# A gated recurrence over a graph on one core: where its states, sums and late rows are kept

## The chip, the core and the metric

The kernel runs on one NeuronCore of a Trainium2 chip. The metric is the device time of one execution in microseconds (us); of several executions the median is taken. The core has TensorE (PE, matmuls, weight loads as PEld), VectorE (DVE), ScalarE (ACT), GpSimd (POOL) and SyncE (SP), which here only issues transfers. A name with q at its end (SPq, ACTq) is the engine's sequencer, which also issues DMAs.

## What is computed

Four graph layers over x [64 batches, 256 nodes, 256 features] and a weighted adjacency [64, 256, 256], each followed by a residual sum and a layer norm. Only layer 0 is touched by the change:

```python
d = adj.sum(-1); norm_adjT = swapaxes(adj, 1, 2) * where(d != 0, 1 / d, 0)[:, :, None]
def step(h, i):                       # i = 0 .. 255, one after the other
    x = h_e[:, i]
    x_par = einsum('bj,bjd->bd', norm_adjT[:, i], h)
    r, z = sigmoid(split(x @ W_ioux.T + b_ioux + x_par @ W_iouh.T + b_iouh))
    hc = tanh(x @ W_coux.T + b_coux + (x_par * r) @ W_couh.T + b_couh)
    return h with row i = z * x_par + (1 - z) * hc
```

h starts as the input, so row i of the sum takes new states for nodes before i and old features (x) for nodes from i on. Layers 1 to 3 are a graph convolution and two attention layers; each batch goes through them alone.

## The kernel before, in words

`_recurrence` does layer 0 and leaves its states in DRAM (Hd); `_layers` does the rest. 64 batches times two halves of 128 features fill the 128 partitions, so that one state, one gate or one sum of a step is a 128x128 tile.

A step n is a chain: the sum xp is transposed on TensorE and copied to SBUF by ScalarE (`flip`, L442 to L447); `h_part` multiplies it by the gate weights; ScalarE forms r (L581), VectorE r times xp (L582); a second flip, a second `h_part`, tanh (L615); then VectorE makes the next sum from c, the gate and what is ready of the sum (v, L600 and L601; xp, L619 and L620). The new state h is formed at the start of the next step (L536, L537).

The sum over nodes is split by age. Time is in blocks of 32 nodes (T), and rounds of 8 (U).

- Pushes. A new state is multiplied by an adjacency weight and added to the sums (ACC) of the nodes in its own round and the next: one instruction of VectorE for a target (`push`, L462), while GpSimd takes the last few targets together (`far`, L566 and L570). The two engines work beside each other. A step has up to 9 pushes of VectorE.
- Late sums. Once a round, TensorE adds what the states of the last 48 or so nodes give to the eight nodes of the round after the next (`late`, L366). It reads a ring Hw in SBUF of 64 rows of states, in two halves of 32 batches. Each state first goes to DRAM (L538); once a round eight rows are read back into the ring (L333). The products are copied (L179) to lb, where a target row lies in one partition, sent to DRAM (Lb, L343), read back (late_sb, L349) in the layout of ACC, and added by GpSimd (L633). The eight rows of a round lie next to each other in each 32 partitions of lb.
- Early sums. For each block, 256 rows times 32 targets of each batch: states older than that and all the old x rows (`early`, L252). They go to DRAM (Eb), and from there to ACC.
- Degrees (`degrees`, L198 to L210) and tables S, An for a block are made one block ahead.

The order of the loop is written out by hand (`manual_schedule`). By p = n % 8: the late matmuls are put in at p = 1 (two pieces after the gates' matmuls) and at p = 2, 3, 4 (one piece ahead of the first gate's matmuls, one behind the second's); early pieces take the same two places at p = 0, 5, 6, 7. Copies wait in a list (`copy_next`), two to a step; loads on ScalarE's queue (L624) and transfers on SP's come at the end of a step. SP sends lb at the end of p = 5 and reads it back at p = 6. GpSimd's addition is put at the end of p = 6, and the first push at p = 7 needs it. Every DMA issue takes one of eight landing counters in turn and waits until the transfer that had it before has landed. [...]four for products and transposes (base), two for rc (the gate r and the candidate c), one for z and one for `flip`.

Of the kernel before, what the change touches and what calls it, by code (L numbers as in the profile page):

```python
# [69 lines left out]
def _recurrence(tc, ident, Hd, x, adj, W_ioux, b_ioux, W_iouh, b_iouh, W_coux, b_coux, W_couh, b_couh):  # L70
# [15 lines left out]

    nc = tc.nc
# [6 lines left out]
    GB = 8  # L94
    NG = B // 4
# [3 lines left out]
    with ExitStack() as ctx:  # L99
# [6 lines left out]
        tri = const.tile([P, T], F32, name="tri")  # L106
# [49 lines left out]
        for s in range(0, P, T):  # L156
            nc.gpsimd.affine_select(
                out=tri[s:s + T], in_=tri[s:s + T], pattern=[[-1, T]], compare_op=ALU.is_ge,
                fill=0.0, base=0, channel_multiplier=1,
            )  # L160

# [3 lines left out]
        dram = ctx.enter_context(tc.tile_pool(name="r_dram", bufs=2, space=bass.MemoryType.DRAM))  # L165
# [3 lines left out]
        copies = []  # L169
        loads = []  # L170
        transfers = {}

        def copy_later(out, in_, then=None):
            copies.append((out, in_, then))

        def copy_next(n):
            if copies:
                out, in_, then = copies.pop(0)
                nc.scalar.copy(out, in_)  # L179
                if then:  # L180
                    then(n)

        def transfer_at(n, f):
            transfers.setdefault(n, []).append(f)

        def base_bank(shape, name):
            return ps.tile(shape, F32, tag="base", name=name, bufs=4)
# [24 lines left out]
        def early_A(k, t, n=None):  # L212

            A = stream.tile([P, 2, 2 * GB, T], F32, tag="A", name=f"A_{k}_{t}")
            g = slice(t * GB, (t + 2) * GB)
            new, own = k * T - W + T // 2, k * T
            for at in range(max(new, 0) // T * T, own, T):
                nc.gpsimd.memset(A[at % P:at % P + T, at // P], 0.0)
            for jc in range(2):
                lo, hi = jc * P, (jc + 1) * P  # L220
                for a, b in ((lo, min(new, hi)), (max(own, lo), hi)):
                    if a < b:
                        nc.sync.dma_start(
                            A[a - lo:b - lo, jc],
                            adj[g, a:b, k * T:(k + 1) * T].rearrange("b j i -> j b i"),
                        )
            def cut():
                part = A[own % P:own % P + T, own // P]
                nc.gpsimd.tensor_mul(  # L229
                    part, part,  # L230
                    tri[own % P:own % P + T].unsqueeze(1).to_broadcast([T, 2 * GB, T]),
                )

            transfer_at(n + 2, cut) if n is not None else cut()
            return A

        def early_H(k, t, queue=False):

            Hs = stream.tile([P, 2, GB, D], F32, tag="Hs", name=f"Hs_{k}_{t}")
            g = slice(t * GB, (t + 1) * GB)  # L240
            new = k * T - W + T // 2
            for jc in range(2):
                lo, hi = jc * P, (jc + 1) * P
                for src, a, b in ((Hd, lo, min(new, hi)), (x, max(new, lo), hi)):
                    if a < b:
                        to, of = Hs[a - lo:b - lo, jc], src[g, a:b, :].rearrange("b j d -> j b d")
                        loads.append((to, of)) if queue else nc.scalar.dma_start(to, of)
            return Hs

        def early_piece(pb, n, jc, t, A, Hs):  # L250
            for q in range(4):
                nc.tensor.matmul(  # L252
                    pb[q * T:(q + 1) * T, n, :], A[:, jc, t % 2 * GB + n * 4 + q, :],
                    Hs[:, jc, n * 4 + q, :], start=(jc == 0), stop=(jc == 1),
                )

        def early_out(Eb, eb, t):
            for q in range(4):
                nc.sync.dma_start(
                    Eb[2 * t - 6:2 * t + 2, q].rearrange("n i d -> i n d"), eb[q * T:(q + 1) * T]  # L260
                )

        def early_in(k, Eb):
            ACC = blk.tile([P, T, P], F32, tag="ACC", name=f"ACC_{k}")
            for c in range(2):
                nc.sync.dma_start(
                    ACC[c * B:(c + 1) * B],
                    Eb.rearrange("n q i d -> (n q) i d")[:, :, c * P:(c + 1) * P],
                )
            tables[k]["ACC"] = ACC  # L270

        def early_Eb(k):
            return dram.tile([NG, 4, T, D], F32, tag="Eb", name=f"Eb_{k}")

        def early_eb(k, t):
            return stream.tile([P, 8, D], F32, tag="eb", name=f"eb_{k}_{t}", bufs=1)

        def early(k):

            Eb = early_Eb(k)  # L280
            n = yield
            A = [early_A(k, 0, n)]
            Hs = [early_H(k, t, True) for t in range(2)]
            n = yield
            for t in range(B // GB):
                m = t * 2 % 8
                if m == 0:
                    eb = early_eb(k, t)
                if t % 2 == 0 and t + 2 < B // GB:
                    A.append(early_A(k, t + 2, n))  # L290
                pb = base_bank([P, 2, D], f"early_{k}_{t}")
                for piece in range(4):
                    early_piece(pb, piece // 2, piece % 2, t, A[t // 2], Hs[t])
                    if piece == 3:
                        then = None
                        if m == 6:
                            def then(n, t=t, eb=eb):
                                transfer_at(n, lambda: early_out(Eb, eb, t))
                                if t == B // GB - 1:
                                    transfer_at(n + 1, lambda: early_in(k, Eb))  # L300
                        copy_later(eb[:, m:m + 2, :], pb, then)
                        if t + 2 < B // GB:
                            Hs.append(early_H(k, t + 2, True))
                    n = yield

        def late_load(k, n=None):

            An = blk.tile([P, HB, T], F32, tag="An", name=f"An_{k}")
            first, last = k * T - W + T // 2, k * T + T // 2
            if first < 0:  # L310
                nc.gpsimd.memset(An, 0.0)
            for lo, hi, at in ring(max(first, 0), last):
                for g in range(2):
                    nc.sync.dma_start(
                        An[g * W + at:g * W + at + hi - lo],
                        adj[g * HB:(g + 1) * HB, lo:hi, k * T:(k + 1) * T].rearrange(
                            "b j i -> j b i"
                        ),
                    )

            def cut():
                nc.gpsimd.tensor_mul(An, An, window[k % 2].unsqueeze(1).to_broadcast([P, HB, T]))

            transfer_at(n + 3, cut) if n is not None else cut()
            return An

        def late(first):
# [3 lines left out]
            for lo, hi, at in ring(max(first - 2 * U, 0), first - U):  # L331
                for g in range(2):
                    nc.sync.dma_start(  # L333
                        Hw[g * W + at:g * W + at + hi - lo],
                        Hd[g * HB:(g + 1) * HB, lo:hi, :].rearrange("b j d -> j b d"),
                    )
            lb = stream.tile([P, NG, D], F32, tag="lb", name=f"lb_{first}", bufs=1)
            Lb = dram.tile([NG, 4, U, D], F32, tag="Lb", name=f"Lb_{first}")
            sides[first] = blk.tile([P, U, P], F32, tag="late", name=f"late_sb_{first}")

            def send():
                for q in range(4):
                    nc.sync.dma_start(  # L343
                        Lb[:, q].rearrange("n i d -> i n d"), lb[q * T + i:q * T + i + U]
                    )
# [8 lines left out]
            def then(n):  # L354
                transfer_at(n, send)
                transfer_at(n + 1, receive)

            yield
            for u in range(0, NG // 2, 2):
                pb = [base_bank([P, 2, D], f"late_{first}_{u}_{g}") for g in range(2)]  # L360
                for e in range(2):
                    for q in range(4):
                        for g in range(2):
# [3 lines left out]
                                pb[g][q * T:(q + 1) * T, e, :], An[rows, b, :], Hw[rows, b, :],  # L367
                                start=True, stop=True,
# [8 lines left out]
                    yield  # L377

        def load_S(k):
# [3 lines left out]
            for c in range(2):  # L383
                nc.sync.dma_start(
                    S[c * B:(c + 1) * B, U - lag:],
                    adj[:, k * T - lag:(k + 1) * T, k * T:(k + 1) * T],
                )
# [15 lines left out]
        def load_x(q):  # L403
            xq = stream.tile([P, Q, P], F32, tag="xq", name=f"xq_{q}")
            for c in range(2):
                nc.sync.dma_start(
# [65 lines left out]
        for k in range(2):  # L472
            for _ in degrees(k):
                pass
# [515 lines left out]
```

## Time and profile before

| what | us |
|---|---|
| median of 3 runs (5433.3 to 5439.5) | 5435.06 |
| the profiled execution | 5423.65 |
| its span | 5421.8 |

The span in three stages, by busy time of the engines, granted TensorE clock and bytes moved:

| stage, us from the start | PE | DVE | ACT | POOL | clock | GB/s |
|---|---|---|---|---|---|---|
| 0 to 182.5: before the first step | 48.6 | 24.3 | 11.2 | 29.5 | 0.82 | 195 |
| 182.5 to 2718.9: the steps | 1546.7 | 1502.7 | 565.5 | 723.3 | 0.79 | 95 |
| 2718.9 to 5421.8: last step's end and the layers | 2446.3 | 1535.0 | 1285.8 | 774.3 | 0.95 | 27 |

A line of a wait names who waited, for what, the total in us, how often and the longest. A line of the timeline has the start, the time it took, the engine, the line and what it writes and reads; what stands in brackets is idle time ahead of it. A line of the chain gives the start and the length of one link of what ended last.

### The profile page before, as it was taken

What the parts mean: (1) busy time and instruction counts of PE and PEld (TensorE: products, weight loads), DVE (VectorE), ACT (ScalarE), POOL (GpSimd) and SP (SyncE); (2) the same over time, 40 slices, a digit from 0 to 9 for tenths busy, and PEclk for the clock granted to TensorE, in tenths of its full rate; (3) what the DMA queues carried; (4) which work ended last, traced back from release to release, by engine and by line L of the source; (5) the groups of instructions that cost most, each with busy time, mean ns of one, the idle gap of its engine ahead of it and who ended that gap; (6) DMA issues with size and microseconds to landing.
All of it is one profiled execution on the core that took longest, in us unless ns stands there. A gap on an engine that the chain in (4) does not pass through costs nothing.

```text
span 5421.8 us, 86877 instructions
## 1 busy us (share of the span) xinstructions
PE 4041.6 (75%) x31904; PEld 2685.1 (50%) x31904; DVE 3062.1 (56%) x9234; ACT 1862.5 (34%) x5755; POOL 1527.0 (28%) x1735
## 2 busy tenths in 40 slices
PE   2566655566565565666669999999999999999998
PEld 1333333333332333333356666666666666666665
DVE  1456656556465564666645655555565555555554
ACT  0122222122121221222234445444444544444454
POOL 1222222223222222232322222222322232232221
PEclk8777778778777787877889999999999999999999
DMA  7434555645545455432110001000000000000000
GB/s 198 100 85 96 110 116 110 125 99 105 115 103 130 94 117 106 98 65 39 32 61 28 24 24 31 25 24 28 28 24 24 30 26 24 28 28 24 24 22 9
DMA packets 571745, 349.86 MB, mean 65 GB/s; under 512 B 200876, under 2 KB 563128, under 8 KB 571320
## 3 DMA queue, kind: packets, MB, share of 16 engines
q1 hardware_dynamic: 449936, 224.23, 19.6%
q10 hardware_dynamic: 121384, 120.08, 8.7%
q8 instruction: 252, 4.13, 0.3%
q14 instruction: 173, 1.42, 0.1%
HBM read 277.49 MB, written 66.58 MB: 63 GB/s over the span
## 4 chain that ended last, share of the span: by engine, by line
PE 40%; DVE 24%; DMA 23%; POOL 4%; ACT 3%; issue 3%; SPq 2%; ACTq 0%; DVEq 0%; POOLq 0%
DVE ACC L462 10%; DMA Hw<-Hd 6%; DMA Lb<-lb 5%; PE tr L720 5%; PE o L909 4%; PE mm_3f L735 3%; DMA late_sb<-Lb 3%; PE rc L429 3%; PE mm_2f L735 2%; PE mm_2k L735 2%; PE mm_2s L735 2%; DMA ad<-in_adj_dram 2%; PE rc L437 2%; PE mm_3q L735 2%; PE mm_2q L735 2%
## 5 line engine op out<-in xcount | busy, mean ns | idle before, releaser
L462 DVE SCALAR_TENSOR_TENSOR ACC<-h,S,ACC 128x128 f32<-128x128 f32 x1867 | 959.2, 571 | 411.3 <-POOL ACC L633 402.3
L750 ACT ACTIVATE sm<-sm,mx 128x256 f32<-128x256 f32 x1152 | 574.4, 500 | 520.8 <-DVE mx L746 509.3
L444 PE MATMUL rT_ps<-ident,r 128*128 128x128 f32 x256 | 95.5, 373 | 650.7 <-DVE r L582 650.6
L566 POOL TENSOR_TENSOR far<-h,S 128x512 f32<-128x512 f32 (+2 forms) x253 | 212.1, 838 | 1211.6 <-DVE h L537 1211.2
L720 PE MATMUL tr<-ident,sm 128*128 128x128 f32 x2304 | 412.5, 303 | 156.5 <-ACT sm L750 155.6
L446 ACT COPY rT<-rT_ps 128x128 f32<-128x128 f32 x256 | 67.9, 265 | 1124.7 <-PE rT_ps L444 1124.0
L720 PEld LDWEIGHTS tr<-ident,sm 128*128 128x128 f32 x2304 | 290.6, 152 | 309.9 <-ACT sm L750 258.9
L746 DVE CUSTOM_DVE_ANT_0 sm<-s,neg 128x256 f32<-128x256 f32 x1024 | 377.4, 416 | 104.7 <-PE s L869 104.7
L444 PEld LDWEIGHTS rT_ps<-ident,r 128*128 128x128 f32 x256 | 38.9, 152 | 778.6 <-DVE r L582 749.8
L366 PE MATMUL late<-Hw,An 64*32 64x256 f32 x3968 | 213.9, 454 | 261.1 <-DMA Hw<-Hd 261.1
L708 POOL TENSOR_TENSOR rstd<-rstd,mhalf 128x2 f32<-128x2 f32 x256 | 179.0, 699 | 767.0 <-DVE rstd L707 594.9
L429 PE MATMUL rc<-WxT,xqT 128*64 128x256 f32 x2048 | 389.2, 465 | 0.0
L909 PE MATMUL o<-pT,v 128*32 128x256 f32 x2048 | 322.5, 410 | 19.4 <-ACT pT L727 14.3
L619 DVE SCALAR_TENSOR_TENSOR xp<-c,Sd,zc 128x128 f32<-128x128 f32 x255 | 89.6, 351 | 434.9 <-ACT c L615 431.5
L727 ACT COPY pT<-tr 128x512 f32<-128x512 f32 x448 | 250.9, 577 | 72.9 <-PE tr L720 72.7
L710 DVE TENSOR_SCALAR y<-y,mv,rstd 128x256 f32<-128x256 f32 x512 | 189.3, 412 | 142.1 <-POOL rstd L708 142.1
L252 PE MATMUL early<-Hs,A 128*32 128x256 f32 x2048 | 170.6, 429 | 126.5 <-POOL A L229 60.6
L570 POOL TENSOR_TENSOR ACC<-ACC,far 128x512 f32<-128x512 f32 (+2 forms) x253 | 252.0, 996 | 19.8
L366 PEld LDWEIGHTS late<-Hw,An 64*32 64x32 f32 x3968 | 59.5, 117 | 332.2 <-DMA Hw<-Hd 286.7
L750 ACT ACTIVATION_READ_ACCUMULATOR sm<-sm,mx 128x1 f32 x1152 | 217.0, 188 | 0.0
L704 DVE BATCH_NORM_STATS2 st<-y 128x6 f32<-128x256 f32 x512 | 194.5, 412 | 17.8 <-POOL y L793 9.9
L437 PE MATMUL rc<-WhT,xpT 128*64 128x128 f32 x2048 | 173.2, 291 | 38.1 <-ACT xpT L446 37.8
(158 smaller groups left out, 8596.3 us busy)
## 6 DMA issues: line engine op xcount, KB each, us to landing
Hs<-in_x_dram ACTq DMA_DIRECT2D x48, 1024.0 KB
rows<-in_adj_dram SPq DMA_DIRECT2D x128, 128.0 KB
xq<-in_x_dram SPq DMA_DIRECT2D x128, 128.0 KB
Eb<-eb SPq DMA_DIRECT2D x64, 256.0 KB
ACC<-Eb SPq DMA_DIRECT2D x16, 1024.0 KB
Hd<-h SPq DMA_DIRECT2D x256, 64.0 KB
Hs<-Hd ACTq DMA_DIRECT2D x16, 1024.0 KB
y<-Hd SPq DMA_DIRECT2D x64, 256.0 KB
```

The lines of the kernel that those rows point to most:

```text
L366: nc.tensor.matmul(pb[g][q * T:(q + 1) * T, e, :], An[rows, b, :], Hw[rows, b, :], start=True, stop=True,)
L429: nc.tensor.matmul(G[o * B:(o + 1) * B], xqT[n // Q][:, n % Q, kc * B:(kc + 1) * B], WxT[:, kc, o, gates], start=False, stop=False, skip_g ...
L437: nc.tensor.matmul(G[o * B:(o + 1) * B], hT[:, kc * B:(kc + 1) * B], WhT[:, kc, o, g], start=False, stop=(kc == 1), skip_group_check=True,)
L462: nc.vector.scalar_tensor_tensor(acc[:, 0, :], h, s, acc[:, 0, :], ALU.mult, ALU.add)
L566: nc.gpsimd.tensor_mul(tmp[:, 0:len(far), :], h.unsqueeze(1).to_broadcast(shape), s.unsqueeze(2).to_broadcast(shape),)
L570: nc.gpsimd.tensor_add(acc, acc, tmp[:, 0:len(far), :])
L720: nc.tensor.transpose(pt[:, a, c * P:(c + 1) * P], src[:, c, a * P:(a + 1) * P], ident)
L727: copy(dst, flipped(src, t))
L735: nc.tensor.matmul(pm[:, c, :], lhsT[:, k, c * P:(c + 1) * P], rhs[:, k, :], start=(k == 0), stop=(k == 1),)
L746: nc.vector.tensor_tensor_reduce(out=dst[:, c, :], in0=src[:, c, :], in1=neg[:, c, :], scale=-scale, scalar=FMAX, op0=ALU.add, op1=ALU.min ...
L750: nc.scalar.activation(dst[:, c, :], dst[:, c, :], AF.Exp, bias=mx, scale=-1.0, accum_out=sums)
L909: nc.tensor.matmul(o_ps[i * HD:(i + 1) * HD], v[:, k, h * HD:(h + 1) * HD], pT[i][:, k, :], start=(k == 0), stop=(k == 1),)
```

## The change

`_layers` is the same. In `_recurrence`:

- The x side of the sums is split off. Ahead of the loop, the products of x with the adjacency are formed for all targets up to node 127 of every batch and written to DRAM (Us); the other half is formed in the first blocks of the loop, at the early places (`x_side`). Early sums now hold states alone, in eight pieces of up to 112 rows (`early`), added by VectorE to a part of Us that is loaded for it and written back. ACC is loaded from Us. Degrees ahead of the loop are made for one block, not for two.
- New states go to the ring within SBUF: ScalarE copies h to hs, and two DMAs write its two feature halves into one row of each half of the ring (`into_ring`). The ring's reload goes. Hd is written from the ring, 32 rows once a block (`flush`). For steps 17 to 20 of a block the writes are held back.
- h, zx and the product sc lie in one PSUM bank (keep); r, c and z are formed in place in PSUM; base has three banks. Each VectorE instruction of a step but the flips' sources has one operand in PSUM. GpSimd no longer forms zx; it forms ready, the finished sum times dinv.
- The late products' columns are arranged so that a round's eight rows lie four partitions apart in lb. late_sb has one buffer.
- Loads of S, An's raw rows, A and Hs wait in one list for ScalarE's queue.

```diff
+        Us = dram.tile([4, N, NG, D], F32, name="Us", bufs=1)
...
+            for g in range(0, B, GB):
...
+                for jc in range(2):
+                    rows = slice(jc * P, (jc + 1) * P)
+                    nc.sync.dma_start(A[:, jc], adj[g:g + GB, rows, 0:P].rearrange("b j i -> j b i"))
+                    nc.scalar.dma_start(Xs[:, jc], x[g:g + GB, rows, :].rearrange("b j d -> j b d"))
...
+                    x_out(0, g + n, 4, ub)
...
+        def sums_in(k, n):
...
+                    nc.sync.dma_start(
+                        ACC[c * B + q:(c + 1) * B:4],
+                        Us[q, k * T:(k + 1) * T, :, c * P:(c + 1) * P].rearrange("i n d -> n i d"),
+                    )
...
+                def add(n):
+                    nc.vector.tensor_add(U_sb[:, m:m + 2], U_sb[:, m:m + 2], pb)
...
         def late(first):
...
-            for lo, hi, at in ring(max(first - 2 * U, 0), first - U):
-                for g in range(2):
-                    nc.sync.dma_start(
-                        Hw[g * W + at:g * W + at + hi - lo],
-                        Hd[g * HB:(g + 1) * HB, lo:hi, :].rearrange("b j d -> j b d"),
-                    )
...
-                        Lb[:, q].rearrange("n i d -> i n d"), lb[q * T + i:q * T + i + U]
+                        Lb[:, q].rearrange("n i d -> i n d"),
+                        lb[q * T + i // U:(q + 1) * T:T // U],
...
                 nc.vector.scalar_tensor_tensor(
-                    acc[:, 0, :], h, s, acc[:, 0, :], ALU.mult, ALU.add
+                    acc[:, 0, :], keep[:, j % 2, :], s, acc[:, 0, :], ALU.mult, ALU.add
                 )
...
+        def flush(lo, hi):
...
+                    nc.sync.dma_start(
+                        Hd[g * HB:(g + 1) * HB, lo:hi, :].rearrange("b j d -> j b d"),
+                        Hw[g * W + at:g * W + at + hi - lo],
+                    )
+
+        def state(n):
+
+            h = keep[:, n % 2, :]
+            zcc = new("zcc", n)
+            nc.vector.tensor_mul(zcc, zc, c)
+            nc.vector.tensor_add(h, zcc, keep[:, 2, :])
+            hs = new("hs", n, 6)
+            nc.scalar.copy(hs, h)
+            ring_in.append((n, hs))
+
+            if not 0 < (n + 1) % T - T // 2 < 5:
+                into_ring()
+            return hs
+
+        def into_ring():
+            while ring_in:
+                n, hs = ring_in.pop(0)
+                for o in range(2):
+                    nc.sync.dma_start(
+                        Hw[n % W::W, :, o * P:(o + 1) * P], hs[o * B:(o + 1) * B]
+                    )
...
-                h = new("h", n - 1, 4)
-                nc.vector.tensor_mul(h, zc, c)
-                nc.vector.tensor_add(h, h, zx)
-                nc.sync.dma_start(Hd[:, n - 1, :].rearrange("b (c f) -> c b f", c=2), h)
+                hs = state(n - 1)
...
+                ready = new("ready", n)
+                nc.gpsimd.tensor_mul(
+                    ready, tables[kk]["ACC"][:, ii, :], dinv[:, n + 1:n + 2].to_broadcast([P, P])
+                )
+            push(3)
...
-            nc.gpsimd.tensor_mul(zx, z, xp)
+            zx = keep[:, 2, :]
+            nc.vector.tensor_mul(zx, Gz, xp)
...
-                nc.vector.scalar_tensor_tensor(v, z, Sd[:, ii:ii + 1], xp, ALU.mult, ALU.mult)
-                nc.vector.scalar_tensor_tensor(
-                    v, tables[kk]["ACC"][:, ii, :], dinv[:, n + 1:n + 2], v, ALU.mult, ALU.add
-                )
-                push(5)
+                nc.vector.scalar_tensor_tensor(v, zx, Sd, ready, ALU.mult, ALU.add)
+                push(4)
+                next_of(sums, n)
...
-                nc.vector.scalar_tensor_tensor(xp, c, Sd[:, ii:ii + 1], zc, ALU.mult, ALU.mult)
-                nc.vector.tensor_add(xp, xp, v)
+                nc.vector.scalar_tensor_tensor(sc, c, Sd, zc, ALU.mult, ALU.mult)
+                nc.vector.tensor_add(xp, sc, v)
...
+            if i == 16:
+                flush(n - T, n)
```

## The prediction

> **What bounds the kernel now.** I read the 40 slices first: the four layers are two stages, and only the first one, the recurrence, is touched. Then when steps start (the operations on xpT_ps), the waits between 200 and 2711 us, one step in the timeline, and the chain of one late round.
>
> ```profile
> PE   2566655566565565666669999999999999999998
> ...
> PEclk8777778778777787877889999999999999999999
> ...
> L462 DVE SCALAR_TENSOR_TENSOR ACC<-h,S,ACC 128x128 f32<-128x128 f32 x1867 | 959.2, 571 | 411.3 <-POOL ACC L633 402.3
> ```
> ```profile
> L444 PE MATMUL xpT_ps<-ident,xp x256: 272/328/476, 182.5 to 2718.9; 128*128 128x128 f32 x128
> ```
> Step 0 starts at 182.5 us, step 255 at 2718.9: 2536.4/255 = 9.95 us a step, 79.6 us per eight. What follows takes 5421.8 - 2718.9 = 2702.9 us.
> ```profile
> POOL ACC L633 <- DMA late_sb<-Lb: 436.8, 31, 20.2
> DVE ACC L462 <- POOL ACC L633: 402.3, 31, 18.2
> ...
> PEld late L366 <- DMA Hw<-Hd: 286.7, 59, 10.1
> ```
> Each eight steps VectorE waits 402.3/31 = 13.0 us for the late sums' return through DRAM (Lb), and TensorE about 286.7/31 = 9.2 us for the ring's reload (Hw).
> ```profile
> 441.46 2.83 DVE L462 SCALAR_TENSOR_TENSOR ACC<-h,S,ACC 128x128 f32<-128x128 f32 x4
> 441.51 0.82 POOL L566 TENSOR_TENSOR far<-h,S 128x384 f32<-128x384 f32 x1 [3.24 <-DVE h L537]
> ...
> 442.41 1.00 POOL L570 TENSOR_TENSOR ACC<-ACC,far 128x384 f32<-128x384 f32 x1
> ...
> 445.06 1.13 DVE L462 SCALAR_TENSOR_TENSOR ACC<-h,S,ACC 128x128 f32<-128x128 f32 x4
> ...
> 453.64 0.33 PE L444 MATMUL xpT_ps<-ident,xp 128*128 128x128 f32 x1
> ...
> 458.85 0.33 PE L444 MATMUL xpT_ps<-ident,xp 128*128 128x128 f32 x1
> ```
> Four pushes take 2.83 us beside GpSimd and 1.13 alone; a step with little on GpSimd takes 5.21 us.
> ```profile
> 454.00 9.60 DMA Lb<-lb
> ...
> 464.31 6.83 DMA late_sb<-Lb
> ...
> 471.30 2.35 POOL ACC L633
> ...
> 482.14 5.10 DMA Hd<-h
> ...
> 487.37 7.30 DMA Hw<-Hd
> ```
> So 79.6 = 22.2 of waits + 57.4, or 7.2 a step: 5.2 clean, 2.0 of stretched VectorE work and half clock.
>
> [...] The trace [...]shows no push with a PSUM operand. [...] 128x512 with a PSUM source (L787) and without (L840) both take 692 ns. I take nothing, at most 0.2 us a step.
>
> **The change, part by part.**
>
> *Start.* Out go two blocks of early sums, two of degrees and Eb; in come the x sums of all 64 batches (8.4 MB of adjacency, 16.8 MB of x, 8.4 MB written to Us), one block of degrees, and 2.1 MB back. About 38 MB against 34 MB, in longer runs, but degrees now queue behind it all. At the 265 GB/s of the best early slices 33.6 MB take 127 us; with 38 us of setup before and 20 for degrees and tables after: 185 us (165 to 230), as before.
>
> *VectorE and GpSimd.* Every push reads h from PSUM, and zcc, h, rx, zx, v, sc and xp have at most one SBUF input. 571 - 347 ns (mean less median) x 1867 = 418 us of VectorE time goes, 1.6 us a step, where the chain waits for VectorE. GpSimd loses zx (0.49 us) and gains ready (same shape). ScalarE gains the copy hs, 0.27 us, beside TensorE's work. A push waits for hs, some 0.3 us; then four pushes (1.1 us) end about 0.4 us after the gate r is there. A step is 4.9 (5.21 less the 0.3 that the gate waited for VectorE at 455.5) + 0.4 + 0.1 for PSUM = 5.4 at full clock. Half clock, about 1.7 us in a step, held some 40% of the recurrence (granted 0.75 to 0.83); I leave 0.3, since 0.7 is the share as before and a clock that is always full gives none. 5.7 x 256 = 1459 us (1360 to 1560).
>
> *Ring.* The DRAM round trip per eight steps (5.10 + 7.30 us, 9.2 of it waited) goes. But in the built order, late matmuls at steps p = 1 to 4 read all 64 ring rows and so wait for the row written in that very step; at p = 2, 3, 4 they stand ahead of the gate matmuls on TensorE. After xp, h takes 0.6 us, hs 0.35, the first of two issues 0.5 (Hd<-h: median 0.534). No trace shows such a transfer within SBUF; Hd<-h took 4.0 to 5.2 us from h, issue included. I bound the second one at 3.0 (half the rows, no DRAM) to 4.5 us from its issue, so 4.45 to 5.95 after xp. Then 0.66 of late matmuls, and gates that would start at 0.9 start at 5.1 to 6.6. I take 4.6 us lost at each of p = 2, 3, 4 and 3.7 at p = 1, where the late work stands behind the gates: 17.5 us. It can't be a gain, since nothing else at these places gets shorter. Of 30 late rounds, 8 (first = 24 within the block) hold their writes back. 22 x 17.5 = 385 us. Late matmuls add 50 us elsewhere on the path.
>
> *Late rows.* [...]the four Lb issues (1.9 us at 452.1) and a last transfer of about 3 us replace 11.5 us from send to landing: 6.5 less. Send to add was 11.5 + 0.7 + 6.8 + 2.35 = 21.4; it becomes 14.9, and 13.0 of waiting becomes 6.5. 30 x 6.5 = 195 us (lower bound 4, upper 13[...]). What is late next is still late_sb.
>
> *Rest.* 64 additions on VectorE (0.69 us, hidden unless tanh is done first), Us traffic that SP waits for, ring writes twice a step on SP, and loads on ScalarE's queue, each held until the transfer eight before has landed; behind them stand the copy xpT and the gates. ScalarE lost about 45 us to this before; 70 (30 to 150).
>
> Sum: 1459 + 385 + 50 + 195 + 70 = 2159 us for the steps, against 2536. With 185 and 2703: 5047 us of span. The profiled execution is 5423.65, with 5421.8 of span, and 11 below the median 5435.06; so 5060, rounded to 5050.
>
> **Rivals.**
> *Ring writes land early and the clock stays up.* For it: they stay in SBUF, with half the rows. Against: a second issue and ScalarE's copy. Steps of 5.3 (-102) and waits of 10.9 a round (-145) give about 4810.
> *VectorE or Lb gains less.* Contention that stays (only steps that don't wait feel it, 168 x 1.2 = 200) or Lb as slow as before (+195): about 5250. [...]
> *The ring's wait takes over: slower.* There are 22 x 4 = 88 waits for this step's own row. SP issues in order, and in front of a ring write may stand Us, rows, or an issue held by the eight-transfer limit; Hw<-Hd took 7 to 17 us on the same queue. 385 us of margin over 88 waits is 4.4 us, so from waits of about 8.8 us instead of 4.4 the kernel loses. At 10.9 us: 5620. Against: Hd<-h, the same kind of row, stayed near 5 us on the chain throughout.
>
> **How the numbers follow.** Forecast 0.53, own range 4900 to 5200; early ring 0.17; less gain 0.19; slower rival 0.11. The range 4830 to 5300 takes in the forecast and the third case, with the bounds of start, steps and late round; it leaves out the slower rival and half the fast one. About 0.2% (11 us) is what a measurement can tell: faster 0.88, same 0.01, slower 0.11.
>
> **What would show it.** Right: pushes with a mean near 350 ns; no Hw<-Hd; a wait of L462 for the late addition near 200 us in all; TensorE's late matmuls waiting for Hw<-hs, four times in three of four rounds, some 300 us and more. Wrong: that wait near nothing (then 4810), or near 800; pushes still at 570; Lb still at 9 us; step 0 beyond 230 us.

## The result, and the profile after

| | before | changed |
|---|---|---|
| median, us | 5434.18 (5430.9 to 5439.5) | 5513.49 (5507.4 to 5525.2) |
| the profiled execution and its span | 5423.65, 5421.8 | 5515.68, 5514.0 |
| step 0 starts, step 255 starts | 182.5, 2718.9 | 153.3, 2791.5 |
| granted clock over the span | 0.867 | 0.854 |

The changed kernel takes 1.0148 times as long (95% interval 1.0128 to 1.0167): slower by 80 us, where 5050 was forecast. The start was shorter by 29 us, what follows the last step longer by 20, and the steps took 2638.2 us instead of 2536.4. The forecast for them was 2159.

From the page after: the slices of TensorE, the chain by line and the pushes.

```profile
PE   5656656546446455676759999999999999999998
...
PE tr L839 5%; DMA Hw<-hs 5%; PE rc L534 4%; PE rc L525 4%; PE late L462 4%; PE o L1028 4%; DMA Us<-Ut 3%; PE mm_3f L854 3%; DMA rows<-in_adj_dram 3%; PE mm_2f L854 2%; PE mm_2k L854 2%; PE mm_2s L854 2%; PE mm_2q L854 2%; PE mm_3q L854 2%; PE mm_3k L854 2%
...
L559 DVE SCALAR_TENSOR_TENSOR ACC<-keep,S,ACC 128x128 f32<-128x128 f32 x1867 | 544.6, 343 | 506.4 <-POOL ACC L753 357.8
```

The first term came out: a push takes 343 ns on average, not 571, and VectorE spends 415 us less on them. But TensorE is less busy in the slices of the steps than before, and three transfers stand in the chain, Hw<-hs (5%), Us<-Ut (3%) and rows (3%), 11% of 5514 us together.

The waits of the changed kernel between 200 and 2800 us (who waited, for what, total us, times, longest):

```profile
PE late L462 <- DMA Hw<-hs: 458.1, 71, 28.1
...
DVE ACC L559 <- POOL ACC L753: 357.8, 30, 33.2
```

The reload's wait (286.7 us before) has become a wait of 458 us for this step's own ring row, once 28 us long; the wait for the late sums' return is 358 us instead of 402, though it was to fall to 195. The same stretch, by SP's own waits:

```profile
SPq L352 <- DMA Us<-Ut: 232.9, 24, 11.2
...
SPq L445 <- DMA Hs<-Hd: 45.3, 8, 5.9
```

24 times SP stands at a load Ut<-Us (L352) until a store Us<-Ut has landed, up to 11.2 us. These are the loads that directly follow a store: Ut has two buffers, and the load takes the one that the store just issued still reads. The other eight of the 32 loads, the first two each time early sums begin anew, find a free buffer and wait for no store. What SP issues after a waiting load stands too. The timeline of step 97 shows what that does; the step begins at 1117.8 and lasts 33.7 us:

```profile
1117.81 0.33 PE L541 MATMUL xpT_ps<-ident,xp 128*128 128x128 f32 x1
...
1119.41 2.68 SPq L387 DMA_DIRECT2D Us<-Ut  x1
1130.72 0.56 SPq L352 DMA_DIRECT2D Ut<-Us  x1
1131.33 2.45 SPq L259 DMA_DIRECT2D rows<-in_adj_dram  x4
1140.97 0.69 DVE L261 TENSOR_REDUCE deg<-rows 128x2 f32<-128x512 f32 x1 [23.26 <-DMA rows<-in_adj_dram]
...
1142.26 0.27 ACT L579 COPY hs<-keep 128x128 f32<-128x128 f32 x1 [23.77 <-DVE keep L577]
...
1142.55 1.21 SPq L590 DMA_DIRECT2D Hw<-hs  x2
...
1145.93 1.96 PE L462 MATMUL late<-Hw,An 64*32 64x256 f32 x32 [26.30 <-DMA Hw<-hs]
```

Read it downwards. The store is issued at 1119.4; the next load waits for it until 1130.7; the degree rows stand behind that load and land at 1140.9; VectorE has their reduction ahead of the new state in its order and has been idle for 23 us; only then come the new state and its copy hs, the ring write, and 2.2 us after its two issues the late matmuls. The waiting list puts these 26 us down to "Hw<-hs", because that came last.

How long the ring takes with nothing ahead is seen from step 216 on, where there are no early sums and no degree rows any more. Chain of the changed kernel, p = 4 of step 220:

```profile
2532.50 0.50 SPq L590
2533.05 2.72 DMA Hw<-hs
2535.91 1.23 PE late L462 x16
2537.13 1.05 PE rc L534 x8
```

From the second issue to the landing 2.72 us, and the late matmuls and the gate after the wait run at half clock: 1.23 and 1.05 us, against 0.59 each in the held step 211; the granted clock is 0.50 from 2535.9 to 2538.2, and 1.00 over the held steps from 2449 to 2472. In these last three unheld rounds steps p = 1 to 4 take 9.7, 11.2, 10.8 and 11.2 us (medians), and 5.2 to 5.7 in the held round.

The starts of the steps, added up by their place in the round, in us (30 rounds have a late round; in 8 of them the changed kernel holds the ring writes back):

| kernel | p = 1 to 4, 22 rounds | of these p = 1 | p = 1 to 4, the 8 held | p = 7, 30 rounds | p = 0, 5, 6 | first 8 and last 7 | sum |
|---|---|---|---|---|---|---|---|
| before | 914 | 465 | 283 | 684 | 552 | 102 | 2536 |
| changed | 1232 | 472 | 179 | 571 | 564 | 92 | 2638 |
| e1_hold | 713 | 337 | 180 | 730 | 565 | 91 | 2278 |
| e7_noearly | 992 | 262 | 180 | 445 | 469 | 90 | 2177 |
| e8_neither | 986 | 254 | 178 | 436 | 459 | 82 | 2142 |
| f1_nout | 1050 | 295 | 178 | 509 | 489 | 90 | 2316 |
| f2_late | 1176 | 405 | 184 | 551 | 495 | 91 | 2497 |
| h1_holdlate | 612 | 210 | 188 | 700 | 489 | 92 | 2080 |

In the changed kernel, where the ring isn't held a round's four steps take 1232/22 = 56.0 us; held they take 179/8 = 22.4. So the waits at the ring, with all that stands ahead of them, cost 33.6 us a round. They are of two kinds. At p = 2, 3 and 4 the 22 rounds take 760 us, and 732 with neither early sums nor rows (e8_neither, below): there the ring's own landing is waited for, whatever else SP carries. At p = 1, the kind of step 97, it is 472 against 254: there the traffic is felt.

### The profile page after: what moved, and what is told of

It reads as the page before. It is cut to its first block, busy times and chain, and to the rows that moved or that the text cites. A ratio compares the mean times of both kernels' runs of the same rounds, so it can differ in the third digit from the quotient of the medians.

```text
span 5514.0 us, 86488 instructions
## 1 busy us (share of the span) xinstructions
PE 4112.2 (75%) x31136; PEld 2775.8 (50%) x31136; DVE 2662.3 (48%) x9315; ACT 1893.2 (34%) x5987; POOL 1471.7 (27%) x1710
## 4 chain that ended last, share of the span: by engine, by line
PE 53%; DMA 21%; DVE 12%; SPq 4%; POOL 3%; ACT 3%; issue 3%; ACTq 0%; POOLq 0%; DVEq 0%
PE tr L839 5%; DMA Hw<-hs 5%; PE rc L534 4%; PE rc L525 4%; PE late L462 4%; PE o L1028 4%; DMA Us<-Ut 3%; PE mm_3f L854 3%; DMA rows<-in_adj_dram 3%; PE mm_2f L854 2%; PE mm_2k L854 2%; PE mm_2s L854 2%; PE mm_2q L854 2%; PE mm_3q L854 2%; PE mm_3k L854 2%
## 5 line engine op out<-in xcount | busy, mean ns | idle before, releaser
L559 DVE SCALAR_TENSOR_TENSOR ACC<-keep,S,ACC 128x128 f32<-128x128 f32 x1867 | 544.6, 343 | 506.4 <-POOL ACC L753 357.8
L681 POOL TENSOR_TENSOR ready<-ACC,dinv 128x128 f32<-128x128 f32 x255 | 102.2, 401 | 1535.5 <-DVE ACC L559 1535.5
L541 PE MATMUL rT_ps<-ident,rx 128*128 128x128 f32 x256 | 98.1, 383 | 414.3 <-DVE rx L707 414.2
L541 PEld LDWEIGHTS rT_ps<-ident,rx 128*128 128x128 f32 x256 | 40.1, 156 | 538.4 <-DVE rx L707 459.3
L740 DVE SCALAR_TENSOR_TENSOR keep<-rc,Sd,zc 128x128 f32<-128x128 f32 x255 | 91.1, 357 | 392.8 <-ACT rc L736 389.5
L707 DVE TENSOR_TENSOR rx<-rc,xp 128x128 f32<-128x128 f32 x256 | 72.5, 283 | 347.1 <-ACT rc L705 346.6
L705 ACT ACTIVATE rc<-rc 128x128 f32<-128x128 f32 x256 | 67.3, 263 | 493.5 <-PE rc L534 492.4
L534 PE MATMUL rc<-WhT,xpT 128*64 128x128 f32 x2048 | 203.3, 329 | 25.7 <-ACT xpT L543 25.6
```

The costliest lines, as they stand in the source:

```text
L534: nc.tensor.matmul(G[o * B:(o + 1) * B], hT[:, kc * B:(kc + 1) * B], WhT[:, kc, o, g], start=False, stop=(kc == 1), skip_group_check=True,)
L559: nc.vector.scalar_tensor_tensor(acc[:, 0, :], keep[:, j % 2, :], s, acc[:, 0, :], ALU.mult, ALU.add)
```

## The experiments

The theory formed from this: the new order on SP's queue took the gain. The forecast priced the ring row, the late rows and the bulk transfers each for itself; the bulk (512 KB pieces of Us, degree rows) stands ahead of both. Rivals: the ring's own wait was mis-sized; the freed VectorE is worth little. "To changed" is the difference of the two ratios times 5434 us. The changed kernel wasn't measured again beside each run, only the kernel before was; with both intervals such a difference is uncertain by 12 to 16 us.

| run | median, us | ratio to before, 95% interval | to changed, us |
|---|---|---|---|
| e1_hold | 5147.6 | 0.9508 (0.9494 to 0.9523) | -348 |
| e2_rows | 5468.7 | 1.0101 (1.0079 to 1.0124) | -26 |
| e3_ut | 5525.2 | 1.0204 (1.0188 to 1.0220) | +30 |
| e4_sbuf | 5595.8 | 1.0331 (1.0314 to 1.0348) | +99 |
| e5_lb | 5636.2 | 1.0384 (1.0366 to 1.0402) | +128 |
| e6_norows | 5438.9 | 1.0024 (1.0014 to 1.0034) | -67 |
| e7_noearly | 5054.2 | 0.9315 (0.9300 to 0.9330) | -453 |
| e8_neither | 5028.3 | 0.9271 (0.9254 to 0.9289) | -477 |
| f1_nout | 5188.4 | 0.9540 (0.9521 to 0.9559) | -330 |
| f2_late | 5381.3 | 0.9896 (0.9882 to 0.9911) | -137 |
| f3_best | 5015.5 | 0.9223 (0.9209 to 0.9237) | -503 |
| f4_best | 5008.2 | 0.9209 (0.9191 to 0.9226) | -510 |
| g1_latestore | 5449.1 | 1.0030 (1.0014 to 1.0045) | -64 |
| g2_order | 5041.1 | 0.9292 (0.9277 to 0.9308) | -465 |
| h1_holdlate | 4959.7 | 0.9150 (0.9129 to 0.9171) | -542 |

**The ring held in every round.**

```diff
-            if not 0 < (n + 1) % T - T // 2 < 5:
+            if not 0 < (n + 1) % U < 5:
                 into_ring()
...
-            if i == T // 2 + 4:
+            if p == 4:
                 into_ring()
```

> Edit: the states of p = 1 to 4 go to the ring together after the late matmuls of p = 4, in every round of eight steps instead of one in four; nothing else. Late matmuls then wait for no row of their own steps. Theory RING (the wait for the step's own ring row, with whatever stands ahead of it on SP, took the gain): in the last block, where nothing else is on SP, the four steps take 9.7, 11.2, 10.8, 11.2 us against about 5 without a wait, so 22.9 us a round and 22 rounds = 500 us go, and up to 250 more where p = 1 took 15 to 36 us: 4760 to 5010 us. Rival QUEUE (SP's order as a whole; the ring is only the first to feel it): the waits come back at the next transfer that is waited for, the late sums' return through Lb at p = 7, and at VectorE's degree reductions: gain below 250 us, 5260 to 5500. Rival OPERAND (VectorE and TensorE gained less than thought, waits are secondary): within 60 us of the changed kernel.

Between the two: 348 us. The steps p = 1 to 4 lose 519 us (1232 to 713), and p = 7 takes 159 back (571 to 730). Step p = 1 still takes 337 us, 15.3 in each of the 22 rounds: VectorE's wait for the rows, ahead of the new state, is still there. By the waits:

```profile
DVE ACC L559 <- POOL ACC L753: 514.3, 30, 33.8
...
DVE deg L261 <- DMA rows<-in_adj_dram: 176.4, 16, 25.3
```

Of the edits that change one thing and leave no work out this gains the most: alone it beats the kernel before by 4.9%. The wait for the late sums' return grows from 358 to 514 us. Eight ring issues in a row now stand ahead of it, and the steps before it are shorter; this run doesn't tell which of the two counts.

**The degree rows spread.**

```diff
-                if p in (0, 6, 7):
+                if i and p in (0, 3, 6):
                     next(background, None)
```

> Edit: the degree rows' reductions are spread to i and p in (0, 3, 6) instead of p in (0, 6, 7), and none stands right behind its own load at a block's first step; so three steps lie between a load's issue and the reduction on VectorE, ahead of the next state. Theory: VectorE's wait for rows (188.7 us in 27 places in the changed kernel's trace) stood on the path at p = 1, since state, copy hs and ring write follow it: 130 to 190 us less, 5320 to 5380. Rival: those steps wait for the ring row behind Us and S on SP's queue in any case, so that the wait is replaced: less than 60 us gained, 5450 or more.

The rival: 26 us, though VectorE's wait for rows fell from 165.8 to 42.4 us in the same stretch. Step p = 1 in the 22 rounds still takes 469 us (472); what it waits for has changed, not how long. Steps p = 0, 5 and 6 gain 81 us, and the held rounds lose 31 of these at p = 1 to 4.

**The traffic with Us through ScalarE's queue.**

```diff
-                nc.sync.dma_start(U_sb, Us[:, k * T:(k + 1) * T, 2 * t:2 * t + 4, :])
+                last.append(load_later(U_sb, Us[:, k * T:(k + 1) * T, 2 * t:2 * t + 4, :]))
...
-                        at_step(n, lambda: nc.sync.dma_start(kept, U_sb))
+                        at_step(n, lambda: nc.scalar.dma_start(kept, U_sb))
```

> Edit: the loads Ut<-Us go through ScalarE's queue with the other early loads, and the stores Us<-Ut are issued by ScalarE instead of SP. Theory QUEUE: in blocks 3 to 5 (392.8, 399.8, 372.8 us against 322 of block 2) SP stands still at Ut<-Us until the store two before has landed, with ring writes and Lb behind it; with the transfers off SP these blocks come near 330 us: 150 to 200 us less, 5310 to 5370, and p = 7 after a held round falls from 33 to 41 towards 25. Rival: ScalarE's sequence now stands at the store and the load instead, with the sigmoid behind, so the blocks stay at 370 or more: within 60 us of the changed kernel, or slower.

A miss for the theory as stated: 30 us slower. The rival has the number but not the reason. ScalarE hardly stands at these transfers (20.4 us in all); SP does, for a store that ScalarE issued:

```profile
SPq L445 <- DMA Us<-Ut: 78.5, 13, 11.3
```

L445 reads Lb back. The landing counters serve both queues (in the changed kernel's trace 1476 issues of SP and 203 of ScalarE take the same eight), and an issue waits for the transfer that had its counter before. SP's loads of x stand for such stores 8 times more (59.7 us), and p = 7 goes from 571 to 644 us. Moving the stores to the other queue didn't free the first one of them.

**The operand back in SBUF.**

```diff
-                    acc[:, 0, :], keep[:, j % 2, :], s, acc[:, 0, :], ALU.mult, ALU.add
+                    acc[:, 0, :], hs_of[j], s, acc[:, 0, :], ALU.mult, ALU.add
```

> Edit, one part undone: the pushes on VectorE read the state from its SBUF copy hs again instead of PSUM; all else as changed. Theory (the operand in PSUM freed VectorE as forecast, but only steps without another wait feel it): pushes 343 ns back to about 570, some 420 us more of busy time, of which the steps p = 0, 5, 6 and the held rounds, about 130 of 256, feel 1.2 us each: 100 to 220 us slower, 5610 to 5730. Rival (the part is worth the full 1.6 us a step): 380 us slower or more, 5890. Rival (hidden in the kernel as it stands): within 40 us, with pushes at 570 all the same; or pushes stay below 400 ns, and then the operand's place isn't the cause of the shorter pushes.

```profile
L559 DVE SCALAR_TENSOR_TENSOR ACC<-hs,S,ACC 128x128 f32<-128x128 f32 x1867 | 829.1, 494 | 487.1 <-POOL ACC L755 343.0
```

494 ns with both operands in SBUF, 343 with one in PSUM: the operand's place is the cause of these 151 ns. That a PSUM operand would take away the longer time beside GpSimd was the forecast's estimate; no trace of before had such a push. The theory had 570; the other 77 ns of the fall from 571 to 343 came with something else in the change, which no run took apart. In the kernel as it stands the operand is worth 99 us, at the theory's lower edge: a step at p = 5 goes from 5.0 to 6.0 us, one that waits for the ring or for Lb doesn't change.

**The late rows next to one another again.**

```diff
-                        lb[q * T + i // U:(q + 1) * T:T // U],
+                        lb[q * T + i:q * T + i + U],
...
-                                An[rows, b].rearrange("p u s -> p (u s)"),
+                                An[rows, b].rearrange("p s u -> p (s u)"),
```

(An is laid out and filled to match.)

> Edit, one part undone: the late sums' eight rows of each batch lie next to one another again (rows q*T+i to q*T+i+7 of lb) instead of four apart; all else as changed. Theory (the spread rows shorten Lb<-lb as forecast, and what is left of p = 7 is the queue ahead of it): Lb<-lb grows by about 6 us and p = 7 with it, in nearly all of the 30 rounds: 150 to 220 us slower, 5650 to 5720 us on this chip, where the changed kernel should stand near 5500. Rival (the queue ahead of Lb hides how long Lb itself takes): within 60 us of the changed kernel.

128 us, below the theory's 150 and far above the rival's 60. The chains of round 216, with little else on SP, show the size of the effect itself. The changed kernel, then e5_lb:

```profile
2548.40 3.23 DMA Lb<-lb
...
2552.43 4.50 DMA late_sb<-Lb
```

```profile
2647.32 8.56 DMA Lb<-lb
...
2656.68 4.46 DMA late_sb<-Lb
```

5.3 us less for the last of the four transfers. Spread over 30 rounds 128 us is 4.3 us a round: in the other rounds a part seems to be hidden.

**Work left out: degree rows, early sums, both.** In e6_norows the loop of `degrees` yields without a load from block 1 on. In e7_noearly the list of early sums is empty (`range(0)`), and ACC is loaded at i = 17 of the block before.

> Left out: the loads of the degree rows and their reductions from block 1 on (the degree is a constant there), so the output isn't the reference's. Theory QUEUE: not only VectorE's wait for the rows goes (spreading it saved 28 us), but also 14 MB in front of the ring writes and of Lb on SP's queue: 100 to 200 us less than the changed kernel's 5500, 5300 to 5400. Rival: the rows only fill time that Us and the ring's own wait take anyway: within 50 us of it.

> Left out: the early sums of blocks 2 to 7 (their loads Hs, A and Ut, their matmuls, the additions and the stores Us<-Ut); the output isn't the reference's. The x side, flush, rows, S and An stay. Theory QUEUE: blocks 3 to 5 (392.8, 399.8, 372.8 us) fall to 300 or below, since SP no longer stands at Ut<-Us (up to 11 us, with ring writes and Lb behind it): 250 to 400 us less, 5100 to 5250. Rival (the blocks are long for the ring's and Lb's own latencies, which stay; early sums fill waiting time): less than 120 us gained. [...]

> Left out: both of these, the degree rows from block 1 on and the early sums; the output isn't the reference's. Theory QUEUE: every block then looks like the last one of the changed kernel, in which SP carries little but ring writes, Lb and x: rounds of 70.2 us, and 51.7 the held one, so 262 us a block, with 2722 after the steps and 153 before them 4970 us, or 5000 with x side and flush; that is, the forecast of 5050 holds for an idle queue, and what failed is its 70 us for the rest. Rival RING (the waits themselves were mis-sized, the queue is secondary): above 5250.

The rows are worth 67 us, between the rival's 50 and the theory's 100. The early sums are worth 453, more than the theory said; the granted clock rose from 0.854 to 0.884 with it. Without both, the kernel takes 5028 us, near the theory's 5000 and far from the rival's 5250, and its steps take 2142 us, where the forecast for the kernel with both was 2159. So the bulk work decides, not the ring's own size; but leaving it out takes away matmuls and VectorE's work too, not transfers alone. Waits of e7_noearly in the same stretch:

```profile
PE late L462 <- DMA Hw<-hs: 266.5, 67, 9.4
...
DVE ACC L559 <- POOL ACC L753: 228.6, 30, 20.8
```

The longest wait for a ring row is 9.4 us instead of 28.1, and the late addition is waited for 229 us instead of 358.

**Which part of the early sums: the round trip, and SP standing at it.** f1_nout drops the loads Ut<-Us and the stores, and copies where it added. f2_late moves all bytes, but issues the load later:

```diff
-                nc.sync.dma_start(U_sb, Us[:, k * T:(k + 1) * T, 2 * t:2 * t + 4, :])
+                def begin(U_sb=U_sb, k=k, t=t, begun=begun, at=n + 3):
+                    nc.sync.dma_start(U_sb, Us[:, k * T:(k + 1) * T, 2 * t:2 * t + 4, :])
+                    begun.append(at)
+
+                at_step(n + 3, begin)
+                last.append(begun)
```

> Left out: only the round trip of the early sums through Us (loads Ut<-Us, stores Us<-Ut); Hs and A are loaded, the matmuls run and VectorE copies their result where it added, so the output isn't the reference's. Leaving the early sums out altogether saved about 450 us. Theory TRIP (32 loads and 32 stores of 512 KB on SP's queue, each load standing until the store before it has landed, are most of that): 300 to 450 us less than the changed kernel's 5500 on this chip, 5050 to 5200. Rival LOADS (Hs and A on ScalarE's queue, 40 MB or so, and the matmuls in front of the gates are most of it): less than 150 us gained.

> Edit: each load Ut<-Us is issued three steps later on SP, when the store before it has landed, all else as changed; SP then doesn't stand at it, and the same bytes move. Theory STAND (SP standing at the load, up to 11 us with ring writes and Lb behind it, is the larger part of the trip's cost): blocks 3 to 5 fall from 373 to 400 us to about 330: 120 to 220 us less, 5280 to 5380. Rival BYTES (the 512 KB pieces themselves in front of the 32 KB ring writes and of Lb on one queue): within 60 us of the changed kernel.

Theory TRIP held: the round trip is 330 of the 453 us. Of theory STAND the number held, 137 us, but not the sentence: standing at the load is less than half of the trip's cost, and blocks 3 to 5 fell to 342 to 355 us, not to 330. In f2_late no wait of SP at Ut<-Us is left (it was 232.9 us).

**Together, and the stores on another queue.** f3_best has the held ring, the late load, and the stores issued by ScalarE; f4_best adds the spread rows and issues S's second copy three steps later; g1_latestore is the late load and the stores on ScalarE without the held ring; g2_order is f3_best with the held rows sent after Lb and x loaded at p = 7; h1_holdlate is only the held ring and the late load.

> Edits: ring writes held to p = 4 in every round (5148 us alone), Ut<-Us issued three steps later, and Us<-Ut issued by ScalarE, which doesn't wait for it. Theory (these are separate costs: the ring's own wait, and the trip on SP's queue): 150 to 300 us less than with the first edit alone, 4850 to 5000. Rival (the first edit has already freed the steps that the trip delayed; what is left is Lb at p = 7): less than 80 us, 5070 or more.

> Edits: as f3_best, and the degree rows' reductions spread to p in (0, 3, 6), and the second copy of S issued three steps after the first, so that SP doesn't stand for it. Theory: with the ring held, nothing takes the place of the wait for rows (176 us in 16 places in the trace with the ring held alone): 60 to 180 us less than f3_best. Rival (as alone, where spreading saved 28 us): within 30 us of f3_best.

> Edits on the changed kernel: Ut<-Us issued three steps later (alone 137 us less than the changed kernel) and the stores Us<-Ut issued by ScalarE, on its queue; the ring isn't held. Theory BYTES (512 KB stores, 11 us each, in front of ring writes and of Lb on SP's queue are most of the other 190 us): 100 to 190 us less than with the late load alone, 5190 to 5280. Rival ([...]ScalarE's queue loses as much): within 40 us of 5381.

> Edits: as f3_best (5016 us), but the held ring rows go at the end of p = 5, behind the issue of Lb, instead of at p = 4 in front of it, and x is loaded at p = 7 instead of p = 4. Theory ORDER (what stands in front of Lb on SP, ten issues of 0.5 to 0.65 us and an x load held by the landing of Hs, makes p = 7 26 to 33 us long): p = 7 falls by about 8 us in some 25 rounds: 150 to 250 us less, 4770 to 4870. Rival (Lb itself, its landing beside Us and Hs, is what takes the time): within 60 us of 5016.

> Edits on the changed kernel: ring writes held to p = 4 in every round, and Ut<-Us issued three steps later; the stores Us<-Ut stay on SP. Theory SUM (the two costs add up: 348 and 137 us alone, as ratios to before 0.064 and 0.025, and the stores' move to ScalarE took some 70 back): ratio 1.0148 - 0.064 - 0.025 = 0.926 at worst, and 0.91 if f3_best's p = 7 of 29 us falls to the 24 us of e1_hold: 4940 to 5030 us. Rival (the late load gains nothing once the ring is held, and the stores' move is what gained in f3_best): near e1_hold, ratio 0.94 or more, 5100 us.

f3_best is 155 us below e1_hold, at the lower edge of its theory. f4_best went with its rival: its further edits gave nothing that can be told from zero (the intervals overlap). g1_latestore fell outside both: the stores on ScalarE's queue cost 73 us against f2_late, as p = 7 goes from 551 to 637 us. Its chain shows why:

```profile
870.45 10.12 DMA Us<-Ut
...
880.59 3.48 DMA late_sb<-Lb
```

SP's read of Lb was issued when a store on the other queue had landed, as in e3_ut; SP's waits there show it 13 times, 81.8 us in all. g2_order landed in its rival's range: p = 7 stayed near 28 us in the loaded blocks and rose from 14.4 to 19 in the last, where the held ring rows now stand between Lb's sending and its reading back. In h1_holdlate the two costs add up, and more: -348 and -137 alone, -542 together. It is the fastest version, 0.915 of the kernel before, so 8.5% faster.

What the long p = 7 of these kernels waits for can be read from h1_holdlate's trace. SP's issues in a loaded round, then in one of the last block, and the wait over all rounds:

```profile
1499.39 12.91 SPq L510 DMA_DIRECT2D xq<-in_x_dram  x2
...
1513.67 2.82 SPq L445 DMA_DIRECT2D Lb<-lb  x4
```

```profile
2076.91 1.34 SPq L510 DMA_DIRECT2D xq<-in_x_dram  x2
...
2079.94 2.83 SPq L445 DMA_DIRECT2D Lb<-lb  x4
```

```profile
SPq L510 <- DMA Hs<-Hd: 136.6, 14, 14.6
```

SP stands at the load of x until a load Hs<-Hd, issued by ScalarE, has landed, and Lb is sent 11 us later than in the other round. In 22 of the 30 rounds p = 7 takes 21 to 36 us, and in each of them SP stands at some issue for a transfer of ScalarE's (Hs, raw or A). In g2_order the same wait met the ring rows, between sending and reading (73.4 us for Hs<-Hd, 87.1 for Us<-Ut), so that run doesn't rule out the queue. No run changed this wait by itself.

## Why the prediction was wrong, step by step

*Start.* Forecast 185, measured 153.3: 32 us better, below its lower bound of 165. The rate was mis-sized: from 38 to 120 us the core moved 336 GB/s, where the forecast took 265. In the experiments it is the same (152.8 to 156.2).

*After the steps.* Taken as unchanged at 2703; it was 2722.5. The last 16 states now go to the ring (2.71 us) and from there to DRAM in one flush, whose landing the layers wait for:

```profile
2796.85 2.71 DMA Hw<-hs
...
2800.06 10.39 DMA Hd<-Hw
```

*VectorE and GpSimd.* Right. 343 ns a push against 347 expected, and steps of 4.9 to 5.8 us where nothing waits; 5.7 for all was a little high. The 0.1 us a step that the forecast left for a PSUM source was its author's estimate, which no trace had shown; at 343 ns a push none of it shows. But e4_sbuf finds the operand alone worth 99 us in a kernel that waits, not 1.6 us in every step.

*Ring.* The mechanism was right to the step: four waits in three of four rounds. Its size failed twice. With the queue free (e8_neither) p = 1 to 4 take 986/22 = 44.8 us against 178/8 = 22.3 held, so 22.5 us a round instead of 17.5: the landing was quicker than bounded (2.7 us from the second issue, not 3.0 to 4.5), but after a wait the late matmuls and gates run at half clock (1.23 and 1.05 us at step 220, against 0.59 each held), which the 4.6 us didn't hold. In the changed kernel it is 33.6 us a round, 739 us in all instead of 385: 15.6 us at p = 1 and 6.0 at each of the other three, where the forecast had 3.7 and 4.6.

*Late rows.* The transfer did what was forecast: a last piece of 3.23 us ("about 3", the author's estimate, which no transfer of the kernel before had shown), and 6 us less at p = 7 of the last block than with the rows undone. But p = 7 in the 30 rounds takes 571 us, or 409 over an unwaited 5.4 us each, where 195 were forecast; 436, so 274, with the queue free. "What is left is still late_sb" was right, and what stands ahead of it on SP wasn't counted.

*Rest.* This is the step that failed: "70 (30 to 150)" for the additions, "Us traffic that SP waits for", ring writes and ScalarE's loads. Measured by leaving out what causes it, early sums and rows cost 2638 - 2142 = 496 us of the steps. Of these, 218 us are at p = 1, 28 at p = 2 to 4, 135 at p = 7, 105 at p = 0, 5 and 6 and 10 in the first and last steps. Against the forecast, 354 us too much are at the ring and 214 at p = 7, with 89 less elsewhere. The sentence named the traffic, but gave each transfer its own small price and no place in the queue: 512 KB pieces, 11 us each, with a load that needs the store before it, on the queue that now carried two transfers a step on which TensorE waits. That the forecast's 2159 matches the 2142 of e8_neither is partly luck: there, the ring was 110 and the late addition 79 above the forecast, and all other terms together 206 below, in a kernel that leaves work out.

*The rivals.* "The ring's wait takes over" was the right kind, named Us and the rows ahead of the ring write, and got a chance of 0.11. It thought of a longer wait at each of the 88 places, 8.8 us from which the kernel loses; they average 8.4, but nearly all the traffic's part is at p = 1. The argument set against it was that Hd<-h stayed near 5 us on the same queue before. SP stood at loads for stores just issued then too, as its waits between 200 and 2800 us show:

```profile
SPq L349 <- DMA Lb<-lb: 152.3, 37, 7.0
SPq L333 <- DMA Hd<-h: 105.2, 30, 4.9
```

But nothing on TensorE needed this step's row, so a state that reached DRAM late was felt once a round at most. A hint lay in the profile of before: its last three full rounds, without early sums and degrees, took 71 to 73 us, those of blocks 1 to 5 78 to 91. The traffic already cost some 10 us a round when the waits on it were fewer.

*Open.* Of the round trip's 330 us, 137 are the standing at the load; the other 193 go with the bytes, but how they split between the place in the queue and the landings that SP waits for wasn't settled: moving the stores made it worse, not better. A third buffer of Ut, which would let the load go ahead with the same bytes, wasn't tried. The 123 us between f1_nout and e7_noearly (Hs, A, matmuls) were not taken apart. That SP's waits for ScalarE's transfers make p = 7 long once the ring is held is read from the traces; no edit has tested it.

## What to carry to other kernels

A latency-critical transfer that was put on SP's queue inherited here the waits of what was issued ahead of it (the ring row: 2.72 us from its second issue to the landing with nothing ahead, a wait of 28.1 us at the longest with the bulk ahead): before pricing such a transfer by its own landing, list what else that queue issues in the same steps, and look for a load that needs a store just issued. When a consumer is given a dependency on the newest data, ask whether it uses it; here the late matmuls multiplied those rows by zeros (the window over An), and two changed lines that hold the writes back turned 1.5% slower into 4.9% faster. Moving the bulk stores to another queue was no way out here, where both queues take the same landing counters: g1_latestore lost 73 us against f2_late. And compare a loaded stretch with an empty one of the same loop in the profile of before: their difference (here 71 to 73 us a round against 78 to 91) is a first price of the traffic that the change is about to put in the way.

## What the runs showed of the hardware

- The second of a pair of 32 KB transfers within SBUF landed 2.6 us after its issue in half of the chain's links through it in e8_neither, 4.3 us at the most; in the changed kernel the middle one is 2.8 and the longest 11.7.
- One PSUM operand took a push from 494 to 343 ns beside GpSimd, the time of an undisturbed one with both in SBUF before (347, the median); no price for the PSUM source showed.
- The last of four transfers out of lb landed 8.56 us after its issue with a round's eight rows side by side, 3.23 with them four partitions apart.
- An issue on SP's queue waited for the landing of a transfer issued on ScalarE's (in the changed kernel Hs<-Hd 45.3 us at the read of Lb; 81.8 us for Us<-Ut in g1_latestore, 136.6 for Hs<-Hd at the load of x in h1_holdlate): in these programs two queues aren't independent.
- After a wait of some 4 us TensorE's matmuls took up to twice as long (1.23 us for 16 late matmuls against 0.59, 1.05 for a gate against 0.59): added up over the pieces of steps 218 to 220, 1.6 to 2.3 us on top of the wait. The granted clock was 0.50 right after it.
